# One table for the order of five engines in the layer loop of a graph network kernel

## The chip, the core and the metric

The kernel runs on one core of a Trainium2 chip. The core has five engines that work side by side: TensorE (PE in the profile, with its weight loads as PEld), VectorE (DVE), ScalarE (ACT), GpSimd (POOL) and SyncE (SP), whose work here is to issue transfers. Each engine takes its instructions strictly from its own queue. The metric is the time of one execution on the device, in microseconds; the time of a kernel is the median of its runs.

## The reference

`x` holds 128 graphs of 64 nodes with 256 features, `adj` one 64x64 matrix for each. Four layers follow each other, and each ends in `x = layernorm(x + layer(x, adj))`:

- Layer 0: five groups of nodes among the first 25, each with two graph convolutions (256 to 512 to 256), fused with softmax weights.
- Layer 1: one symmetric normalised graph convolution.
- Layer 2: a polynomial of degree 3 in the row-normalised adjacency, times a linear map, then a leaky ReLU.
- Layer 3: five rounds of message passing with a GRU cell. This is most of the work:

```python
A = (adj != 0)
for l in range(5):
    m   = einsum('bnd,de->bne', h, weight[l])
    agg = einsum('bij,bid->bjd', A, m)
    gi, gh = agg @ w_ih.T + b_ih, h @ w_hh.T + b_hh      # three gates of 256 columns
    r, z = sigmoid(i_r + h_r), sigmoid(i_z + h_z)
    n = tanh(i_n + r * h_n)
    h = (1 - z) * n + z * h
```

Everything is float32.

## The kernel before

**Chunks and steps.** The 128 graphs form 16 chunks of 8; two graphs lie together in 128 partitions, so a chunk has four such pairs. Layer 0 runs first, over all graphs, with layers 1 and 2 of chunks 0 and 1 woven in. Then comes the layer 3 loop. Two chunks are in work at a time and alternate: step s does one round of the chunk `rows[s % 2]`. Ten steps, a *period*, take two chunks through five rounds. There are 79 steps in the loop; a last one is written out behind it. In steps 8 and 9 of a period the chunks are in their last round.

**Products of a step.** The gate products use a fast scheme with seven block products instead of eight. `Gates.product(i)` issues product i; 1, 6, 7 and 4 accumulate in one PSUM bank a, 2 in bank b, 5 and 3 in bank d. Between them ACT copies bank a out (`c`, L794), and DVE adds such a copy to bank b or d (L796, L800, L806). Before product 6 can write into bank a, the copy c1 must have read it, and so on for 7 and 4. There is one such set for the gates r and z (`parz`, `pbrz`, `pdrz`) and one for n (`pan`, `pbn`, `pdn`). Products 5, 6, 7 and 4 read sums of the operands that POOL makes in `sums` (L757 to L759: `Th` of the state, `Ta` of the message).

**The rest of a step.** `sigmoid` (L871) runs on ACT; `reset` (L934, L935) on DVE, tanh (L940) on ACT, then three operations of `update` (L941 to L943) on DVE. `new(i)` does reset, tanh and update for one quarter of the state. `flip` turns half of a new state around: a DVE transpose (L918), one write to DRAM (L923), four reads back (L927), both issued by SP. `messages` gathers the neighbours on PE (L224), copies on ACT (L226) and makes `Ta`. `state_by_transfer` (L829 to L846) brings the next chunk's state into its transposed form, through DRAM as well. `output` and `close` add the result to x, normalise (L152) and store it.

**Filler.** `mid(c)` does layers 1 and 2 of a later chunk. It is a generator; each `next(filler)` in `step` issues it up to its next `yield`. There are nine pieces to a chunk, and two places for them in most steps.

**What sets the order.** In the loop PE, ACT, SP and POOL issue in the order in which `step` is written. DVE is left to the scheduler of the language, which builds a fixed order from priorities (`tc.high_priority()`) and estimates when the kernel is built. The centre of `step` is:

```python
        x.rz(1)
        if w: w.new(3)
        if closing: closing.close()
        ...
        x.rz(2); x.rz(5)
        if s % (2 * L): next(filler, None)
        x.rz(6); x.sigmoid(2)
        x.n(1); x.n(2); x.rz(7); x.new(2)
        ...
        x.rz(3)
        if w and w.l < L - 1: w.messages()
        ...
        x.sigmoid(3); x.new(7); x.n(4); x.n(3); x.new(4)
```

Of the kernel before, what the change touches and what calls it, by code (L numbers as in the profile page):

```python
# [25 lines left out]
H = CB * N // 2  # L26
# [39 lines left out]


@with_exitstack
def gnn_stack(
# [45 lines left out]
    def inv_sqrt(v, n, p, name):  # L115

        s = small.tile([p, n], F32, name=name + "s")
        nc.vector.scalar_tensor_tensor(s, v, 0.0, v, op0=ALU.is_equal, op1=ALU.add)
        r = small.tile([p, n], F32, name=name + "r")
        powers.append(nc.gpsimd.tensor_tensor(r, s, mhalf[:p, :n], ALU.pow))  # L120
        o = small.tile([p, n], F32, name=name + "o")
        nc.vector.scalar_tensor_tensor(o, v, 0.0, r, op0=ALU.not_equal, op1=ALU.mult)
        return o

# [109 lines left out]
    def mid(c, first=False):  # L234
# [3 lines left out]
        with tc.issue_after(evictions[-1].ins):  # L238
            for two in range(2):
                b = slice(two * N, (two + 1) * N)  # L240
                nc.vector.transpose(AT1[b, :, b], aB[b])
        nc.vector.tensor_scalar(A01, Ab, 0.0, None, op0=ALU.not_equal)
        rsum = small.tile([128, NP], F32, name="rsum")
        with tc.issue_after(evictions[-1].ins):
            nc.vector.tensor_reduce(rsum, Ab, AX.X, ALU.add)
        rdeg = small.tile([128, NP], F32, name="rdeg")
        nc.vector.tensor_scalar(rdeg, rsum, 1.0, None, op0=ALU.add)
        rinv = small.tile([128, NP], F32, name="rinv")
# [3 lines left out]
        nc.vector.tensor_scalar(rsum, rsum, 1e-9, None, op0=ALU.add)  # L252
        dg = keep.tile([128, NP, 128], F32, name="dg", bufs=1)
        nc.vector.tensor_mul(
            dg, ident[:, None, :].to_broadcast([128, NP, 128]), rsum[:, :, None].to_broadcast([128, NP, 128])
        )
        An = keep.tile([128, NP, 128], F32, name="An", bufs=1)
# [4 lines left out]
        poly = keep.tile([128, NP, 128], F32, tag="poly", name="poly3", bufs=2)  # L262
        nc.scalar.activation(poly, dg, AF.Identity, scale=cw[:, 2:3])
        dinv1 = inv_sqrt(rdeg, NP, 128, "d1")
        with tc.high_priority():
            nc.vector.scalar_tensor_tensor(poly, AT1, cw[:, 3:4], poly, op0=ALU.mult, op1=ALU.add)

# [5 lines left out]
        xt = xts.pop(c)  # L273
        p = psum("pp").rearrange("p (q n) -> p q n", q=NP)
        for q in range(NP):
            nc.tensor.matmul(p[:, q, :], An[:, q, :], poly[:, q, :], start=True, stop=True)
        poly = keep.tile([128, NP, 128], F32, tag="poly", name="poly1", bufs=2)
        with tc.high_priority():
            nc.vector.scalar_tensor_tensor(poly, dg, cw[:, 1:2], p, op0=ALU.mult, op1=ALU.add)
        ag = gather(halves(xt), AT1, "ag1")  # L280
        if not first:
            yield
        nc.vector.tensor_add(xt, xt, l1bs[:, None, :].to_broadcast([128, NP, D]))
        p = psum("pp").rearrange("p (q n) -> p q n", q=NP)
        for q in range(NP):
            nc.tensor.matmul(p[:, q, :], An[:, q, :], poly[:, q, :], start=True, stop=True)
        poly = keep.tile([128, NP, 128], F32, tag="poly", name="poly0", bufs=2)
        with tc.high_priority():
            nc.vector.scalar_tensor_tensor(poly, dg, cw[:, 0:1], p, op0=ALU.mult, op1=ALU.add)
        yield  # L290
        for u in range(NP // 2):
            p = psum("pd").rearrange("p (q d) -> p q d", q=2)
            for h in range(2):
                q = 2 * u + h
                for k in range(2):
                    nc.tensor.matmul(  # L296
                        p[:, h, :], ag[:, k, q * 128 : (q + 1) * 128], L1W[:, k, :], start=k == 0, stop=k == 1
                    )
            for h in range(2):
# [3 lines left out]
                )  # L303
        norm = norm_stats(xt)
        yield
        norm_apply(xt, *norm_root(*norm))
# [5 lines left out]
        for u in range(NP // 2):  # L312
            p = psum("pd").rearrange("p (q d) -> p q d", q=2)
            for h in range(2):
                q = 2 * u + h
                for k in range(2):
                    nc.tensor.matmul(
                        p[:, h, :], ag[:, k, q * 128 : (q + 1) * 128], L2W[:, k, :], start=k == 0, stop=k == 1
                    )
            v = keep.tile([128, 2, D], F32, name="v", bufs=1)  # L320
            for h in range(2):
                q = 2 * u + h
                nc.scalar.activation(v[:, h, :], p[:, h, :], AF.Identity, bias=cb, scale=rinv[:, q : q + 1])
            nc.vector.scalar_tensor_tensor(v, v, 0.2, v, op0=ALU.mult, op1=ALU.max)
            nc.vector.tensor_add(xt[:, 2 * u : 2 * u + 2, :], v, xt[:, 2 * u : 2 * u + 2, :])
        norm = norm_stats(xt)
        yield
        norm_apply(xt, *norm_root(*norm))
# [433 lines left out]
    class Gates:  # L762
# [22 lines left out]
        def product(self, i):  # L785
            C = self.C
            if i == 1:
                self.a = self.bank("a")
            if i in (1, 6, 7, 4):
                self.multiply(self.a, i)  # L790
                if i != 4:
                    c = self.copies[i] = work.tile([128, 2, H], F32, tag="copy", name=f"c{i}", bufs=4)
                    with tc.high_priority():
                        nc.scalar.copy(c, self.a)  # L794
                if i == 7:
                    nc.vector.tensor_add(C[:, :, 1, H:], self.d, self.copies.pop(7))  # L796
            elif i == 2:
                b = self.bank("b")
                self.multiply(b, i)
                nc.vector.tensor_add(C[:, :, 0, :H], b, self.copies.pop(1))  # L800
            else:
                if i == 5:
# [413 lines left out]
```

## Time and profile before

| | |
|---|---|
| median of 3 runs | 2202.35 us (2202.05 to 2204.06) |
| the profiled execution | 2206.19 us, span in the trace 2204.1 us |
| layer 0, first part of the span | up to about 345 us |
| 79 steps of layer 3 | 344.6 to 2171.3 us |
| last step and output | 2171.3 to 2204.1 us |
| mean clock granted to PE | 0.99 |

The profile is one execution. Its span reaches from the first to the last instruction; the 2.1 us between span and time lie around it. A row of the list of instructions names source line, engine, operation, the tile written and those read, a count, busy time and the mean duration of one. Behind it may stand the engine's idle time just before, with what ended it. Neighbouring matmuls overlap, so that PE's busy time is no measure of its idle moments alone; the distance from one start to the next is.

### The profile page before, as it was taken

The page shows a single profiled execution, that of the slowest core. Times are in us where ns is not written, and L with a number is a line of the kernel's source. Part 1 is how long each engine was busy: PE and PEld are TensorE (multiplying, and loading weights), DVE is VectorE, ACT ScalarE, POOL GpSimd, SP SyncE. Part 2 cuts the span into 40 slices and gives each one's busy share as a digit, 9 for nine tenths or more (in the row PEclk, how much of TensorE's full clock was granted, in tenths as well). Part 3 has the DMA queues.
Part 4 walks back from the last instruction along what each step waited for, and adds up shares of the span by engine and source line. Part 5 has one row for each costly group of instructions (what it writes and reads, how often), then busy time and mean ns, then how long its engine had stood idle before and what let it go on. Part 6 is the DMA issues. An engine that isn't in the chain of part 4 may idle for free.

```text
span 2204.1 us, 31432 instructions
## 1 busy us (share of the span) xinstructions
PE 2117.5 (96%) x10738; PEld 1832.8 (83%) x10738; DVE 1603.6 (73%) x3881; ACT 974.3 (44%) x2006; POOL 605.0 (27%) x635
## 2 busy tenths in 40 slices
PE   9989999999899999999999989999999999999997
PEld 6667788888788887888788878888888888888886
DVE  3344665777888688877887777869787788778666
ACT  3323334444444444444444444444444444454444
POOL 3311121232323213322222232323222233323222
PEclk9989999999999999999999999999999999999999
DMA  6632110222322242223331332224221332223221
GB/s 164 180 107 67 32 47 20 55 56 58 77 72 53 53 77 77 60 52 72 72 77 39 77 67 77 52 50 86 65 66 39 78 78 66 55 61 74 61 58 39
DMA packets 521994, 149.76 MB, mean 68 GB/s; under 512 B 488702, under 2 KB 516860, under 8 KB 521836
## 3 DMA queue, kind: packets, MB, share of 16 engines
q1 hardware_dynamic: 516996, 142.58, 26.6%
q0 software_dynamic: 2128, 4.77, 0.9%
q8 instruction: 85, 1.39, 0.3%
q10 hardware_dynamic: 2712, 0.42, 0.1%
q14 instruction: 73, 0.60, 0.1%
HBM read 82.67 MB, written 65.01 MB: 67 GB/s over the span
## 4 chain that ended last, share of the span: by engine, by line
PE 64%; DVE 18%; DMA 5%; SPq 4%; ACT 4%; issue 2%; POOL 2%; ACTq 0%; DVEq 0%; POOLq 0%
PE parz L777 16%; PE pan L777 9%; PE pdrz L777 8%; PE pa L224 7%; PE pdn L777 4%; PE pbrz L777 4%; PE ps L468 3%; PE ph L452 3%; DMA hb<-flip 3%; PE pd L296 3%; DVE NI L934 2%; PE pbn L777 2%; DVE RZ L941 2%; DVE NI L935 2%; DVE RZ L942 1%
## 5 line engine op out<-in xcount | busy, mean ns | idle before, releaser
L777 PE MATMUL parz<-Th,WHH 128*128 128x256 f32 x960 | 291.1, 385 | 26.5 <-ACT c L794 26.5
L940 ACT ACTIVATE NI<-NI,bih 128x256 f32<-128x256 f32 x316 | 159.9, 506 | 349.0 <-DVE NI L935 348.6
L777 PE MATMUL parz<-Ta,V 128*128 128x256 f32 x960 | 288.4, 382 | 0.0
L757 POOL TENSOR_TENSOR Ta<-agg 128x512 f32<-128x512 f32 x80 | 103.0, 1288 | 642.3 <-ACT agg L226 642.3
L794 ACT COPY c<-parz 128x512 f32<-128x512 f32 x240 | 139.5, 581 | 272.2 <-PE parz L777 272.0
L871 ACT ACTIVATE RZ<-RZ,brz 128x256 f32<-128x256 f32 x474 | 215.1, 504 | 46.1 <-DVE RZ L800 31.6
L777 PEld LDWEIGHTS parz<-Th,WHH 128*128 128x128 f32 x960 | 180.4, 192 | 57.6 <-ACT c L794 34.4
L777 PEld LDWEIGHTS parz<-Ta,V 128*128 128x128 f32 x960 | 184.5, 192 | 25.8
L140 POOL TENSOR_TENSOR rs<-ve,mhalf 128x4 f32<-128x4 f32 (+2 forms) x65 | 68.3, 1051 | 368.4 <-DVE ve L133 301.2
L757 POOL TENSOR_TENSOR Th<-hn 128x512 f32<-128x512 f32 x64 | 81.4, 1272 | 319.9 <-DVE hn L943 289.0
L226 ACT COPY agg<-pa 128x512 f32<-128x512 f32 x160 | 93.7, 586 | 162.8 <-PE pa L224 162.8
L777 PE MATMUL pan<-Ta,V 128*128 128x256 f32 x474 | 146.4, 391 | 19.4 <-ACT c L794 18.9
L794 ACT COPY c<-pan 128x512 f32<-128x512 f32 x237 | 136.4, 576 | 33.5 <-PE pan L777 32.3
L777 PE MATMUL pan<-Th,WHH 128*128 128x256 f32 x474 | 142.1, 382 | 0.0
L942 DVE TENSOR_TENSOR RZ<-RZ 128x256 f32<-128x256 f32 x316 | 139.1, 442 | 2.7
L934 DVE SCALAR_TENSOR_TENSOR NI<-NI,bhh,RZ 128x256 f32<-128x256 f32 x237 | 130.4, 550 | 4.1
L224 PEld LDWEIGHTS pa<-A,h 128*128 128x128 f32 x1024 | 126.2, 193 | 6.6 <-issue 3.0
L224 PE MATMUL pa<-A,h 128*128 128x128 f32 x1024 | 127.4, 277 | 2.5 <-DMA h<-hb 2.5
L941 DVE TENSOR_TENSOR RZ<-hn,NI 128x256 f32<-128x256 f32 x252 | 106.2, 421 | 18.4 <-ACT NI L940 17.4
L935 DVE TENSOR_TENSOR NI<-NI 128x256 f32<-128x256 f32 x237 | 113.1, 477 | 3.2
L777 PEld LDWEIGHTS pan<-Ta,V 128*128 128x128 f32 x474 | 80.7, 192 | 38.4 <-ACT c L794 32.6
L943 DVE TENSOR_TENSOR hn<-RZ,NI 128x256 f32<-128x256 f32 x256 | 108.7, 444 | 2.3
(231 smaller groups left out, 4815.2 us busy)
## 6 DMA issues: line engine op xcount, KB each, us to landing
hb<-flip SPq DMA_DIRECT2D x184, 256.0 KB
h<-hb SPq DMA_DIRECT2D x624, 64.0 KB
out_dram<-xt SPq DMA_DIRECT2D x30, 256.0 KB
hT<-hb SPq DMA_DIRECT2D x112, 64.0 KB
W<-in_w_dram SPq DMA_DIRECT2D x10, 512.0 KB
xt<-xb SPq DMA_DIRECT2D x32, 156.0 KB
xo<-in_x_dram SPq DMA_DIRECT2D x9, 512.0 KB
xb<-xo SPq DMA_DIRECT2D x9, 512.0 KB
```

What stands on the lines that cost most here:

```text
L224: nc.tensor.matmul(p[:, q * 128 : (q + 1) * 128], src(q, k), m[:, q, :], start=True, stop=True)
L226: nc.scalar.copy(a[:, k, :], p)
L757: nc.gpsimd.tensor_sub(t[:, 0:2, :], a[:, :, H:], a[:, 0, :].rearrange("p (s n) -> p s n", s=2))
L777: nc.tensor.matmul(bank[:, g, :], w[:, q, i - 1, :], rhs, start=i in (1, 2, 5) and g == 0 and m == 0, stop=m == len(side) - 1, skip_group_ ...
L794: nc.scalar.copy(c, self.a)
L871: nc.scalar.activation(v, self.g.a[:, q, :] if i == 4 else v, AF.Sigmoid, bias=brz[:, 2 * q + j : 2 * q + j + 1])
L934: nc.vector.scalar_tensor_tensor(n[:, j, f], h, bhh[:, 4 + j : 5 + j], r[:, j, f], op0=ALU.add, op1=ALU.mult)
L935: nc.vector.tensor_add(n[:, j, f], i, n[:, j, f])
L940: nc.scalar.activation(n, n, AF.Tanh, bias=bih[:, 4 + j : 5 + j])
L941: e.tensor_sub(d, self.hT[:, j, f], n)
L942: e.tensor_mul(d, d, z)
L943: e.tensor_add(self.hn[:, j, f], d, n)
```

## The change

The pieces of a step get one-letter names, and a table `ORDERS` lists them in order for each kind of step: "8", "9", "0" and "1" for those places in a period, "p" for the six others. `step` walks through the list. DVE joins the engines whose order is fixed in the loop. A capital letter is the chunk of this step (x), a small one that of the step before (w):

- R, N: gate products (r and z; n). r, n: their copies on ACT. A, B: their sums on DVE.
- S: sigmoid. X, T, U or x, t, u: reset, tanh and update, which `new` had in one. f: a flip with its write. d: the four reads.
- G: messages. e and h: POOL's sums of the state. y: state transfer. l: loads. p: one piece of filler.

`mid` yields 19 times a chunk in the loop instead of nine. Its roots on POOL, and poly3 on ACT, are issued earlier. `output` becomes a generator of four pieces, the last with the normalisation and the store, and goes ahead of `mid` at the places p. The message gather stands behind products N4 and N3 where it stood ahead of them. Both flips stand in the next step. Chunks 0 and 1, in layer 0, keep 16 places.

```diff
+ORDERS = {
+    "p": """
+u3 l u4 t7 R1 h r1 R2 p u7 R5 f0 f1 e R6 d0 y r6 A2 d1 N1 N2 n1 B2 S2 p R7 X2
+N6 r7 n6 T2 p N5 A7 S7 R4 N7 n7 U2 p R3 N4 B7 S4 A3 N3 X7 B3 S3 X4 G X3 T3 p T4
+""",
+    "8": """
+R1 t7 l u4 r1 R2 u7 A2 R5 u3 p f0 f1 R6 d0 N1 d1 N2 r6 h n1 B2 p e y S2 R7 r7
+N6 N5 p X2 n6 T2 A7 R4 N7 n7 p S7 R3 N4 B7 A3 N3 S4 G X7 X4 B3 S3 U2 X3 p T4 T3
+""",
+    "9": """
+u3 h l R1 R5 t7 R2 u7 u4 r1 A2 f0 d0 p f1 R6 r6 N1 N2 p n1 S2 d1 p B2 X2 R7 r7
+e N6 n6 N5 A7 T2 N7 y R4 S7 n7 S4 U2 p R3 B7 N4 N3 G A3 X7 S3 B3 p X4 X3 T4 T3
+""",
+    "0": """
+u4 R1 h r1 u3 t7 R2 R5 u7 p R6 f0 f1 A2 N1 r6 d0 l d1 n1 y N2 S2 R7 N6 p B2 N5
+X2 r7 n6 A7 R4 T2 N7 n7 p U2 p B7 e R3 S7 A3 X7 N4 N3 S3 S4 B3 X4 T4 G X3 p T3
+""",
+    "1": """
+u4 u3 R1 h t7 R2 R5 p u7 l f0 r1 R6 e r6 f1 d1 N1 n1 N2 A2 B2 d0 S2 p R7 r7 N6
+X2 n6 T2 N5 A7 R4 N7 n7 p U2 B7 p y R3 S7 A3 N4 S4 X7 N3 S3 G B3 X4 X3 T4 T3 p
+""",
+}
...
         rdeg = small.tile([128, NP], F32, name="rdeg")
         nc.vector.tensor_scalar(rdeg, rsum, 1.0, None, op0=ALU.add)
+        root = inv_sqrt_begin(rdeg, NP, 128, "d1")
...
         norm = norm_stats(xt)
+        norm = norm_root(*norm)
         yield
-        norm_apply(xt, *norm_root(*norm))
+        norm_apply(xt, *norm)
...
+        def copy(self, i):
+            c = self.copies[i] = work.tile([128, 2, H], F32, tag="copy", name=f"c{i}", bufs=4)
+            with tc.high_priority():
+                nc.scalar.copy(c, self.a)
+
+        def sum(self, i):
+            v = self.C[:, :, 1, H:] if i == 7 else self.C[:, :, 0, :H] if i == 2 else self.C[:, :, 0, H:]
+            nc.vector.tensor_add(v, self.b if i == 2 else self.d, self.copies.pop({7: 7, 2: 1, 3: 6}[i]))
...
+        def update(self, i):
+            j, f = self.part(i)
+            n, d, z = self.NI[:, 1, j, f], self.RZ[:, 0, j, f], self.RZ[:, 1, j, f]
+            nc.vector.tensor_sub(d, self.hT[:, j, f], n)
+            nc.vector.tensor_mul(d, d, z)
+            nc.vector.tensor_add(self.hn[:, j, f], d, n)
...
+                if q % 2:
+                    yield
+            norm = norm_stats(self.xt)
+            norm = norm_root(*norm)
+            yield
+            mv, rs, _ = norm
+            nb = small.tile([128, NP], F32, name="nb")
+            nc.vector.scalar_tensor_tensor(nb, mv[:, :, 0], -1.0, rs, op0=ALU.mult, op1=ALU.mult)
+            self.norm = mv, rs, nb
+            self.close()
+            yield
...
+    def piece():
+        while outputs:
+            try:
+                return next(outputs[0])
+            except StopIteration:
+                outputs.pop(0)
+        next(filler, None)
...
+        for o in ORDERS[{8: "8", 9: "9", 0: "0", 1: "1"}.get(s % (2 * L), "p")].split():
+            k, i = o[0], int(o[1:] or 0)
+            if k in do:
+                do[k](i)
+            elif k == "e" and w:
+                w.end()
...
+            elif k == "p":
+                piece()
...
+            elif k == "G" and w:
+                if w.l < L - 1:
+                    w.l += 1
+                    w.messages()
+                else:
+                    if nxt:
+                        nxt.messages()
+                        rows[(s + 1) % 2] = nxt
+                    outputs.append(w.output())
         before = x

-    ordered = {mybir.EngineType.Activation, mybir.EngineType.SP, mybir.EngineType.Pool}
+    ordered = {
+        mybir.EngineType.Activation, mybir.EngineType.SP, mybir.EngineType.Pool, mybir.EngineType.DVE,
+    }
```

The updates of the loop's last step that are still due stand behind the first product of the last step, as a group.

## The prediction

> **What bounds the kernel now.** I read the busy shares first, then the waits of PE, then the table of busy time by stretch for one ten-step period of layer 3, and last the timelines around the largest wait.
>
> ```profile
> PE 2117.5 (96%) x10738; PEld 1832.8 (83%) x10738; DVE 1603.6 (73%) x3881; ACT 974.3 (44%) x2006; POOL 605.0 (27%) x635
> ...
> PE parz L777 <- ACT c L794: 26.5, 17, 2.6
> PE pan L777 <- ACT c L794: 18.9, 23, 2.0
> PE pT L419 <- DVE A L411: 15.3, 2, 14.4
> PE pdrz L777 <- POOL Ta L757: 7.6, 6, 1.5
> PE pa L224 <- DMA h<-hb: 2.5, 2, 2.3
> ```
>
> PE is the bound, and what can be gained is PE's waiting (total, times, longest). Of its five lines only the third lies in layer 0. Layer 3 loses time to copies out of the accumulating bank that ACT makes late, and to POOL's sums Ta.
>
> ```profile
> 1300.38:1329.01 28.63, 24.83 (x126) 21.43 (x124) 23.43 (x56) 12.35 (x26) 10.26 (x11) 0.94 0.32 85
> ...
> 1400.02:1419.94 19.92, 19.92 (x102) 17.75 (x100) 14.77 (x32) 9.89 (x21) 6.59 (x8) 1.00 0.22 53
> ...
> sum 234.78, PE 227.54 PEld 200.84 DVE 186.22 ACT 108.26 POOL 67.69; mean PE 22.75 PEld 20.08 DVE 18.62 ACT 10.83 POOL 6.77
> ```
>
> The rows are steps 41 and 45 (length, then busy PE, PEld, DVE, ACT, POOL, then clock). Step 45 has no filler on PE and runs at PE's floor, 19.92 us. Step 41 has 2.7 us of filler products, so a floor of 22.6, and takes 28.6 at a lower clock. To size this I took all starts of matmuls from PE's timeline: 256 columns follow each other at 0.215 us, 128 columns at 0.112. Whatever a distance exceeds that by is lost. By place in the period (step number modulo 10) a step loses on average 0.9 (0), 5.0 (1), 0.8 (2), 1.4 (4) and 2.6 us (9), and nothing (under 0.06) in 3, 5, 6, 7 and 8. **Summed over steps 0 to 78 that is 83.3 us; it is the most that this change can win in the loop.**
>
> Step 51 shows the mechanism, first on PE, then ACT, then DVE:
>
> ```profile
> 1545.13 0.59 PE L777 MATMUL pbn<-hT,WHH 128*128 128x256 f32 x2
> 1548.30 1.22 PE L777 MATMUL parz<-Th,WHH 128*128 128x256 f32 x2 [2.57 <-ACT c L794]
> 1549.31 1.06 PE L777 MATMUL parz<-Ta,V 128*128 128x256 f32 x2
> ```
> ```profile
> 1543.10 0.51 ACT L940 ACTIVATE NI<-NI,bih 128x256 f32<-128x256 f32 x1 [5.38 <-DVE NI L935]
> 1545.09 2.07 ACT L152 ACTIVATE xt<-xt,nb,rs 128x256 f32<-128x256 f32 x4 [1.49 <-DVE nb L144]
> 1547.07 0.70 ACT L263 ACTIVATE poly<-dg,cw 128x512 f32<-128x512 f32 x1
> 1547.68 0.56 ACT L794 COPY c<-parz 128x512 f32<-128x512 f32 x1
> ```
> ```profile
> 1543.63 0.42 DVE L941 TENSOR_TENSOR RZ<-hT,NI 128x256 f32<-128x256 f32 x1 [0.57 <-ACT NI L940]
> 1544.09 0.43 DVE L942 TENSOR_TENSOR RZ<-RZ 128x256 f32<-128x256 f32 x1
> 1544.56 0.43 DVE L943 TENSOR_TENSOR hn<-RZ,NI 128x256 f32<-128x256 f32 x1
> ```
>
> ACT's queue is fixed. The copy that frees bank a for product 7 stands behind a tanh that waits for DVE, four normalisations of a finished chunk that wait for DVE's nb, and poly3. PE stops for 2.6 us.
>
> [...] the pairs after this wait start 1.01, 0.85 and 0.86 us apart instead of 0.43, some 1.8 us more. [...] here dependent L941, L942, L943 start 0.46 apart and independent ones 0.335, so only dependence costs. [...] the mean L934 is 550 ns against 470 where POOL is idle, and over a step's 20 gate operations the means exceed the quiet values by about 0.8 us.
>
> **The change, part by part.** No engine gains or loses an instruction; orders alone differ. So PE's floor stays.
>
> Filler in small pieces: a chunk of layers 1 and 2 becomes 19 pieces and an output 4, 46 per period, for 50 places (5 "p" per step). Pieces fall in a fixed sequence, so each step's load follows. A DVE base step is 12.95 us (busy in step 73, no filler); four updates as uninterrupted triples add (0.46-0.335)x2 x4 = 1.0, of which I count 0.5 since old orders held some too: 13.4. Pieces, from their rows: half an output 4x0.26 = 1.05; statistics 4x(0.32+0.08)+0.16 = 1.75; A01 1.27; row sums 1.5; dg and An 1.67; d1o and poly 0.9; AT 1.5; power 0.73; bias 1.2; product half 0.88; apply 4x0.32 = 1.3; leaky half 1.5; state transfer 1.3. DVE's load beside PE's floor (19.92 plus 1.72 per product half, 1.8 per gather, 0.9 per power) in steps 0 to 9:
>
> - 0: 18.7 / 19.9; 1: 19.5 / 19.9; 2: 17.8 / 22.6; 3: 18.9 / 24.2; 4: 18.2 / 25.2
> - 5: 20.1 / 19.9; 6: 17.6 / 23.5; 7: 18.2 / 25.2; 8: 20.8 / 23.4; 9: 15.8 / 19.9
>
> Before, DVE worked 23.4 us in step 1, 23.0 in step 4. Now only 0, 1 and 5 are full, and step 9 comes before 0 with 4 us free.
>
> Deadlines: with PE's marks (R 1.72 us, N 0.86, message gather 1.8), order p needs product 7's copy before R4 at 12.0, so S2 ahead of it needs A2 by 10.4; and n7 before N4 at 16.3, so S7 ahead of it needs A7 by 14.5. DVE enters each step late: B3 waits for N3 at 18.1, and B3 0.65, X4 0.85, X3 0.85 and a last piece of 1.7 end at 22.1, 2.2 us into the next step. Summed on from there (u3 u4 2.5, piece, u7 1.25, flips 1.3, A2 0.65) A2 ends at 8.8 in step 2 and 9.2 in step 5; B2, A01, X2, row sums and A7 end at 14.1 in step 5. The spare is 0.4 to 1.6 us, and POOL's locks, 0.8 a step, eat it over two steps running. I take 0.5 lost after step 1 and 1.3 in 5 and 6; the ends are 0 and 3 each.
>
> Closing: normalise and store sit in a piece behind n7, no longer ahead of c6. The 2.1 us on ACT now lie in front of S7, S3, S4 and the message copies: in step 0 these end at 21.2 against 20.4 wanted, 0.8 us, and 0.2 in step 1. The two output transfers wait on SP behind the period's fetches, with nothing behind them until the next step's flips.
>
> Roots (POOL's pow) start one piece before their reader: covers the 46.2 and 41.9 us of DVE waits on POOL d1r and rs, off PE's path, counted in the above.
>
> State transfer y: that of step 49 had its write issued by SP only at 1522.14, 8 us into step 50, and hT landed at 1535.17, when POOL's Th, then Ta, ran late. Now it follows A7 in step 9, about 13 us in; 13 us later is 6 to 7 us into step 0. POOL's queue there holds Th (2.9 us), so Ta of the message at 20 is not behind it: the 1.5 us waits go.
>
> Flips and fetches: SP issues both writes, then both reads. From the first flip: 0.4 + 0.4, 2.2 to land, 4 reads 1.8, again 1.8, landing 1.9 (a late gather at 2046.68 after issue ended 2044.82) = 8.4. First flip at 8.6 makes 17.0 against the gather at 18.1: hidden. If DVE is a further microsecond late, nothing hides it.
>
> Messages move behind N4 and N3: 1.72 us less cover for Ta. Gather end + copy 0.8 + Ta 1.3 to 1.4 = 2.2, needed at 3.9: hidden, except in step 9, where R5 precedes R2 (needed at 2.15): 0.2.
>
> Banks: R1 follows B2's bank, R2 S4's, N5 A2's, all earlier than the copies. Layer 0 keeps its 16 places, and the tail does three updates (3.8 us) under 7 us of products: 0, at most 2 us either way.
>
> Left over: 7 periods x (0.8+0.2+0.5+1.3+0.2 = 3.0) = 21, slow clock after these about 1: **22 us. Gain 83.3-22 = 61.** The profiled execution took 2206.2 (span 2204.1, 2.1 around it), so 2145; the median stands 3.8 lower: 2141.
>
> **Rivals.**
> 1. Nothing is left of the waits (spare is larger than I sum, since POOL's locks are already in my means): 2202.4-83.3 = 2119. For it: seven steps in ten have margin; against: step 5 holds 20.1 in 19.9.
> 2. The arrears of the full steps carry on: 1, 5 and 6 lose 2 more each, 7x6 = 42: gain 19, 2183.
> 3. **Slower.** DVE's order is fixed, and nothing passes a waiting instruction. In orders p and 9 the copy n7 stands on ACT behind S7, and S7 behind A7 on DVE, which follows X2 and a piece. If that chain reaches N4 late in ordinary steps too, 7 steps in 10 pay, 55 in all. It decides from 83.3/55 = 1.5 us per step; with 2.0 it is 110-83 = 27 slower, 2229. For it: the spare of step 5 is 0.4; against: steps 2, 4, 6, 7 and 9 have 4 to 7 us free.
> 4. The flips' reads land after the gather: a delay of 0.5 in 79 steps is 40, gain 43 - 22 = 21, 2181.
>
> **How the numbers follow.** Forecast (2125 to 2165) 0.60, rival 1 0.15, rivals 2 and 4 together 0.14, rival 3 0.09, no change 0.02. The 80% range leaves out rival 3 and half a tail of 1: 2119 to 2183. Faster by over 0.2% (4.4 us, about what a measurement of this kernel can tell from no change) 0.89, within 0.02, slower 0.09.
>
> **What would show it.** Right: steps 0, 1, 5 and 9 take 20 to 21.5 us and 2 to 4 and 6 to 8 their floors above; parz's wait on c falls below 5 us, pdrz's on Ta below 2; the state transfer's write is issued inside step 9. Wrong: waits of pan on c in every step (rival 3), of pa on h<-hb (rival 4), or parz on ACT agg in all steps.

## The result, and the profile after

In this measurement the kernel before took 2203.2 us (median of 4 runs, 2202.05 to 2204.68), the changed one **2172.67 us** (4 runs, 2170.48 to 2174.68). The ratio is 0.9861, 95% interval 0.9844 to 0.9878. The gain is 30.5 us, half of the 61 us forecast. The time lies 8 us above the forecast's own range (2125 to 2165), inside the 80% range (2119 to 2183), and 8 to 10 us below the numbers of rivals 4 and 2 (2181 and 2183).

The page of the changed kernel, busy shares first, and its waits of PE (total, times, longest):

```profile
PE 2109.4 (97%) x10738; PEld 1825.9 (84%) x10738; DVE 1708.3 (79%) x3881; ACT 980.6 (45%) x2006; POOL 600.4 (28%) x635
```
```profile
PE pT L464 <- DVE A L456: 14.7, 1, 14.7
PE pdrz L822 <- DVE RZ L846: 11.9, 14, 1.6
PE pdn L822 <- DVE NI L846: 8.7, 14, 2.2
PE pan L822 <- ACT c L842: 4.6, 6, 0.8
PE parz L822 <- ACT agg L255: 3.7, 6, 0.9
PE parz L822 <- ACT c L842: 2.9, 3, 2.2
```

Instruction counts are those of before. The two waits on copies, 26.5 and 18.9 us, are down to 2.9 and 4.6; the wait on Ta (7.6) and the one on the flips' reads (2.5) are gone. In their place stand waits that before did not have: `pdrz` and `pdn` on DVE's sums. These are products R3 and N3, which write bank d and must wait until the sums A7 and B7 have read it. Line numbers have shifted: L777 is now L822, the copies are L842, the sums L846, reset L977 and L978, update L940 to L942.

The table of busy time by stretch, for steps 41, 45 and 50 (length, then busy PE, PEld, DVE, ACT, POOL):

```profile
1285.89:1305.80 19.91, 19.91 (x102) 17.74 (x101) 18.61 (x48) 10.71 (x23) 7.76 (x8) 1.00 0.30 80
1378.26:1399.28 21.02, 20.46 (x102) 17.50 (x101) 20.31 (x52) 10.22 (x21) 7.61 (x8) 1.00 0.21 51
1492.43:1515.00 22.57, 20.46 (x103) 17.58 (x102) 21.30 (x48) 11.68 (x25) 6.89 (x7) 1.00 0.58 123
```

Step 41, which took 28.6 us, is at PE's floor. Step 45 lost nothing before and now loses 1.1. Step 50, place 0 of its period, loses 2.6.

Counted as in the prediction (distance between starts of matmuls beyond 0.215 or 0.112 us; one of 256 columns is listed with 0.38 us, as neighbours overlap), the loop loses 47 us instead of 83. By place in the period, averages: 2.8 (0), 0.7 (1), 0.1, 0.1, 0.3, 0.8 (5), 0, 0.1, 0, 1.1 (9). From the first to the last step the loop is 35.9 us shorter. The tail behind it, from step 79 on, takes 36.9 us instead of 32.8. Together that is the 31.8 us between the spans 2204.1 and 2172.3.

### The profile page after: what moved, and what is told of

The parts are those of the page before. It is cut to its first block, busy times and chain, and to the rows that moved or that the text cites. A ratio compares the mean times of both kernels' runs of the same rounds, so it can differ in the third digit from the quotient of the medians.

```text
span 2172.3 us, 31481 instructions
## 1 busy us (share of the span) xinstructions
PE 2109.4 (97%) x10738; PEld 1825.9 (84%) x10738; DVE 1708.3 (79%) x3881; ACT 980.6 (45%) x2006; POOL 600.4 (28%) x635
## 4 chain that ended last, share of the span: by engine, by line
PE 76%; DVE 14%; DMA 3%; POOL 2%; ACT 2%; SPq 2%; issue 1%; POOLq 0%; DVEq 0%; ACTq 0%
PE parz L822 19%; PE pdrz L822 10%; PE pan L822 10%; PE pa L253 8%; PE pdn L822 5%; PE pd L323 5%; PE pbrz L822 5%; PE ps L513 4%; PE ph L497 3%; PE pbn L822 2%; DVE xt L184 2%; DVE NI L977 1%; DVE RZ L940 1%; PE pp L312 1%; DVE RZ L941 1%
## 5 line engine op out<-in xcount | busy, mean ns | idle before, releaser
L842 ACT COPY c<-parz 128x512 f32<-128x512 f32 x240 | 138.4, 577 | 365.3 <-PE parz L822 365.3
L802 POOL TENSOR_TENSOR Ta<-agg 128x512 f32<-128x512 f32 x80 | 111.4, 1393 | 693.2 <-ACT agg L255 693.2
L822 PE MATMUL parz<-Th,WHH 128*128 128x256 f32 x960 | 286.8, 380 | 2.9 <-ACT c L842 2.9
L822 PE MATMUL parz<-Ta,V 128*128 128x256 f32 x960 | 286.0, 380 | 0.0
L822 PEld LDWEIGHTS parz<-Th,WHH 128*128 128x128 f32 x960 | 180.8, 190 | 29.5 <-ACT c L842 2.7
L822 PEld LDWEIGHTS parz<-Ta,V 128*128 128x128 f32 x960 | 182.7, 190 | 24.9
L935 ACT ACTIVATE NI<-NI,bih 128x256 f32<-128x256 f32 x316 | 148.7, 503 | 98.1 <-DVE NI L978 96.1
L842 ACT COPY c<-pan 128x512 f32<-128x512 f32 x237 | 138.1, 583 | 105.3 <-PE pan L822 105.3
L941 DVE TENSOR_TENSOR RZ<-RZ 128x256 f32<-128x256 f32 x316 | 157.4, 498 | 10.7
L846 DVE TENSOR_TENSOR NI<-pdn,c 128x512 f32<-128x512 f32 x158 | 108.6, 687 | 55.3 <-ACT c L842 47.7
L940 DVE TENSOR_TENSOR RZ<-hn,NI 128x256 f32<-128x256 f32 x252 | 128.4, 509 | 26.8 <-ACT NI L935 26.6
L822 PE MATMUL pan<-Ta,V 128*128 128x256 f32 x474 | 141.7, 381 | 4.6 <-ACT c L842 4.6
L822 PE MATMUL pan<-Th,WHH 128*128 128x256 f32 x474 | 141.0, 379 | 0.0
L977 DVE SCALAR_TENSOR_TENSOR NI<-NI,bhh,RZ 128x256 f32<-128x256 f32 x237 | 126.4, 533 | 8.2 <-ACT RZ L920 5.0
L846 DVE TENSOR_TENSOR RZ<-pdrz,c 128x512 f32<-128x512 f32 x160 | 109.5, 685 | 29.0 <-PE pdrz L822 24.2
L942 DVE TENSOR_TENSOR hn<-RZ,NI 128x256 f32<-128x256 f32 x256 | 120.6, 471 | 9.1
```

The costliest lines, as they stand in the source:

```text
L802: nc.gpsimd.tensor_sub(t[:, 0:2, :], a[:, :, H:], a[:, 0, :].rearrange("p (s n) -> p s n", s=2))
L822: nc.tensor.matmul(bank[:, g, :], w[:, q, i - 1, :], rhs, start=i in (1, 2, 5) and g == 0 and m == 0, stop=m == len(side) - 1, skip_group_ ...
L846: nc.vector.tensor_add(v, self.b if i == 2 else self.d, self.copies.pop({7: 7, 2: 1, 3: 6}[i]))
L935: nc.scalar.activation(n, n, AF.Tanh, bias=bih[:, 4 + j : 5 + j])
L940: nc.vector.tensor_sub(d, self.hT[:, j, f], n)
L941: nc.vector.tensor_mul(d, d, z)
```

## What is left of the waits: POOL's sums stretch DVE

Step 50 shows how the 2.6 us come about. DVE at the step's start, then POOL, in the changed kernel:

```profile
1493.66 1.19 DVE L977 SCALAR_TENSOR_TENSOR NI<-NI,bhh,RZ 128x256 f32<-128x256 f32 x1 [0.22 <-ACT RZ L920]
1494.88 0.83 DVE L978 TENSOR_TENSOR NI<-NI 128x256 f32<-128x256 f32 x1
1495.63 0.95 DVE L940 TENSOR_TENSOR RZ<-hn,NI 128x256 f32<-128x256 f32 x1
1496.62 0.43 DVE L941 TENSOR_TENSOR RZ<-RZ 128x256 f32<-128x256 f32 x1
```
```profile
1493.29 1.27 POOL L802 TENSOR_TENSOR Ta<-agg 128x512 f32<-128x512 f32 x1 [15.25 <-ACT agg L255]
1494.64 0.79 POOL L803 TENSOR_TENSOR Ta<-agg,Ta 128x256 f32<-128x256 f32 x1
1495.51 0.79 POOL L804 TENSOR_TENSOR Ta<-agg,Ta 128x256 f32<-128x256 f32 x1
```

Three DVE operations stand beside POOL's three, and each ends about 0.3 us after the POOL operation that it met. They take 2.97 us instead of 1.32 (0.48, 0.42, 0.42 below). DVE has no wait in which to make this up: from 1493.66 to 1508.63, where A7 ends, it is busy for 14.4 of 15.0 us. Just ahead of A7 it loses 1.2 us more beside POOL's Th (a 128x4 operation of the statistics takes 0.98 us instead of 0.17, a reset sum 0.83 instead of 0.42). PE waits 1.41 us for A7.

Two experiments settle that POOL's sums are the cause. In the first POOL makes no sums at all; in the second it makes them and nobody reads them:

```python
def sums(a, name): return None                      # no_sums
rhs = {..., 4: a[:, 1, :H], 5: a[:, 0, H:], 6: a[:, 1, H:], 7: a[:, 1, :H]}[i]   # both
```

**no_sums.**

> The changed kernel without POOL's sums Th and Ta (products 4 to 7 read the operand's own halves instead, so the outputs are not the reference's): POOL is left with the pow operations alone, and PE, ACT and DVE do the same number of instructions in the same order. Theory P (what is left of PE's waits comes from POOL: its sums keep DVE's two-input operations and the normalisations waiting, and so DVE enters steps 0, 1, 5 and 9 late): lost time in the loop falls from 47 us to below 15, gate operations all at 0.42 to 0.48, about 2135 to 2145 us. Theory O (the arrears come from the order itself: S3 behind the message copies, a piece ahead of X4 and X3, the writes behind the reads): lost time stays above 35 us, 2160 to 2172.

Measured: 2139.2 us (4 runs), ratio to before 0.9703 (0.9688 to 0.9717); 16 us lost in the loop, tail 33.6. Theory P holds: the time is in its range, the loss just above the 15 us that it allowed. DVE in the same place of step 50 of this kernel (L973, L974, L936 are the same three operations):

```profile
1473.39 0.48 DVE L973 SCALAR_TENSOR_TENSOR NI<-NI,bhh,RZ 128x256 f32<-128x256 f32 x1 [0.22 <-ACT RZ L916]
1473.91 0.42 DVE L974 TENSOR_TENSOR NI<-NI 128x256 f32<-128x256 f32 x1
1474.25 0.42 DVE L936 TENSOR_TENSOR RZ<-hn,NI 128x256 f32<-128x256 f32 x1
```

**sums_unread.**

> The changed kernel with POOL's sums Th and Ta written but not read (products 4 to 7 read the operand's own halves, so the outputs are not the reference's). POOL works as much and at about the same places as in the changed kernel, but no product waits for it. Theory K (POOL's sums cost by what they do to DVE[...]): like the changed kernel, 2165 to 2175 us, loss in the loop over 40 us. Theory D (products wait for Ta and Th, directly or by the order behind them): like the kernel without sums, 2138 to 2148.

Measured: 2173.6 us (4 runs), 0.9856 (0.9842 to 0.9871), over 50 us lost in the loop. It is the changed kernel again, waits included:

```profile
PE pdrz L822 <- DVE RZ L846: 11.5, 14, 1.7
PE pdn L822 <- DVE NI L846: 10.1, 13, 3.8
PE pan L822 <- ACT c L842: 4.6, 6, 0.8
```

Theory K holds: no product waits for Ta or Th, directly or behind something else, and the 34 us between the two runs come from POOL's work. It could cost in one other way: on POOL's queue the roots (pow) stand behind the sums, and DVE waits for roots. In the loop it does so for 6.5 us in the changed kernel, 8.1 in sums_unread and 0.9 in no_sums. Against that, DVE is busy for 1197.6 us in steps 10 to 69 of the changed kernel and for 1093.3 in no_sums, with the same instructions. So the stretched operations are by far the larger part.

Which operations suffer is seen in the groups of DVE's instructions with shapes kept apart (busy us, then mean ns). First the changed kernel, then no_sums:

```profile
L941 DVE TENSOR_TENSOR RZ<-RZ 128x256 f32<-128x256 f32 x316 | 157.4, 498 | 10.7
L977 DVE SCALAR_TENSOR_TENSOR NI<-NI,bhh,RZ 128x256 f32<-128x256 f32 x237 | 126.4, 533 | 8.2 <-ACT RZ L920 5.0
L184 DVE TENSOR_SCALAR xt<-xt,mv,rs 128x256 f32<-128x256 f32 x130 | 71.2, 608 | 6.5 <-POOL rs L169 5.7 <-POOL rs L1031 0.8
L977 DVE SCALAR_TENSOR_TENSOR NI<-pan,bhh,RZ 128x256 f32<-128x256 f32 x79 | 37.5, 475 | 0.0
```
```profile
L937 DVE TENSOR_TENSOR RZ<-RZ 128x256 f32<-128x256 f32 x316 | 134.2, 425 | 10.7
L973 DVE SCALAR_TENSOR_TENSOR NI<-NI,bhh,RZ 128x256 f32<-128x256 f32 x237 | 113.3, 478 | 12.5 <-ACT RZ L916 9.4
L184 DVE TENSOR_SCALAR xt<-xt,mv,rs 128x256 f32<-128x256 f32 x130 | 44.8, 407 | 6.5 <-POOL rs L169 5.6 <-POOL rs L1027 0.9
L973 DVE SCALAR_TENSOR_TENSOR NI<-pan,bhh,RZ 128x256 f32<-128x256 f32 x79 | 37.6, 476 | 0.1
```

The reset with both inputs in SBUF takes 478 ns on average without POOL's sums and 533 with them; in the changed kernel the 35 that overlap a sum take 862, the 202 others 476. The one that reads its input from PSUM (`pan`) takes 475 to 476 ns in both, but there none overlaps a sum. Before, 68 of its 79 did: these take 479 ns, the 11 others 470. The normalisation L184 has one large input and goes from 407 to 608. Why one form is stretched and another not, the runs don't show. What the prediction and the expectations call POOL's lock is this stretch.

I summed it: for each DVE instruction in the loop that overlaps one of POOL's sums, its duration less the median of its own kind beside no sum. That gives 66 us under Ta and 26 under Th before, and **112 and 22 in the changed kernel**, together 1.7 us a step. The change raised it without one instruction more. These are groups of before, to set beside L184, L941 and L977 above: the normalisation and the update's product have grown, the reset has not.

```profile
L155 DVE TENSOR_SCALAR xt<-xt,mv,rs 128x256 f32<-128x256 f32 x130 | 46.4, 407 | 42.7 <-POOL rs L140 41.9 <-POOL rs L996 0.8
L942 DVE TENSOR_TENSOR RZ<-RZ 128x256 f32<-128x256 f32 x316 | 139.1, 442 | 2.7
L934 DVE SCALAR_TENSOR_TENSOR NI<-NI,bhh,RZ 128x256 f32<-128x256 f32 x237 | 130.4, 550 | 4.1
```
The reason is where the sums lie. Before, the gather stood ahead of N4 and N3, and Ta ran beside reset 4 (from PSUM), sum B3 (from PSUM) and the transposes (0.48, 0.68 and 0.71 us on average beside a sum, 0.47, 0.68 and 0.70 beside none). Now Ta runs over reset 3, the updates and the normalisations.

**gather_early** tests that reason. The gather is put back ahead of N4 in all five sequences, all else as changed; sequence p:

```diff
-R3 N4 B7 S4 A3 N3 X7 B3 S3 X4 G X3 T3 p T4
+R3 G N4 B7 S4 A3 N3 X7 B3 S3 X4 X3 T3 p T4
```

> The message gather goes back ahead of N4 and N3 in all five orders; all else stays. Theory G (the late gather costs: the agg copy waited for in step 1, R5 in step 9, and POOL's Ta lies on the updates at the next step's start): the wait of parz on ACT agg (3.7 us) goes and DVE's operations are blocked less, 4 to 10 us faster, 2163 to 2169. Rival H (the late gather is needed for the fetched state): waits of pa on h<-hb appear, 0.3 to 0.8 us a step, 2190 to 2220. My own prediction had the move at nearly nothing: within 4 us of 2172.7.

Measured: 2196.8 us (12 runs), 0.9973 (0.9964 to 0.9982); 75 us lost in the loop. The stretch falls to 34 us under Ta and 20 under Th, so the gather's place does set it. But rival H holds, and neither theory G nor my own prediction, for PE now waits elsewhere; its waits in this kernel:

```profile
PE pa L253 <- DMA h<-hb: 14.0, 8, 2.6
PE pdrz L822 <- DVE RZ L846: 10.9, 14, 1.7
PE parz L822 <- ACT c L842: 8.6, 20, 1.1
```

Of the 14.0 us of waits on the flips' reads 13.8 lie in step 1 of the periods. The late gather gives the reads and the copies their time and is worth 24 us in all, although it puts Ta over DVE's worst operations.

**g_mid** puts G between N4 and N3 in sequence p, that is in steps 2 to 7 (`N4 B7 S4 A3 N3 X7 B3 S3 X4 G X3` becomes `N4 B7 S4 A3 G N3 X7 B3 S3 X4 X3`).

> The changed kernel with the message gather of sequence p (steps 2 to 7) between N4 and N3 rather than behind N3, 0.9 us earlier. Ta then lies over B3 and X4, which read PSUM, and the locks of these steps fall (over all steps 112 us of stretched DVE operations under Ta, 34 with the gather ahead of N4). If lock and reads are both as I read them, steps 2 to 7 gain little, as they lose only 1.45 us between them, and the earlier gather meets the flips' reads in some: between 3 us faster and 8 us slower than the changed kernel. If the gather's late place is worth what it is (24 us) mainly in p steps: over 10 us slower.

Measured: 2187.1 us, 0.9925 (0.9911 to 0.994), 14 us worse than the changed kernel. The stretch under Ta fell to 80 us as expected, yet the loss rose, most in step 5 (0.8 to 1.9): the second case of the expectation holds. The reads are not the reason here, PE waits only 0.9 us for them. The gather now stands ahead of N3, so N3 and its sum B3 end 1.8 us later, and DVE enters the next step that much later: A2 ends 12.4 us into step 5 instead of 10.5, and PE waits for it with product N5, whose bank it frees. B3 of step 44 in the changed kernel:

```profile
1376.68 0.69 DVE L846 TENSOR_TENSOR NI<-pdn,c 128x512 f32<-128x512 f32 x1 [0.18 <-PE pdn L822]
```

and in g_mid, with the new wait of PE:

```profile
1387.24 0.69 DVE L846 TENSOR_TENSOR NI<-pdn,c 128x512 f32<-128x512 f32 x1 [1.97 <-PE pdn L822]
PE pdn L822 <- DVE RZ L846: 6.4, 6, 1.1
```

So a part of what the late gather is worth is that it lets N3, and with it DVE, go first.

## What the gain lives from

**dve_free** takes DVE out of the fixed order again: `ordered = {Activation, SP, Pool}`, with table and pieces as changed.

> The changed kernel with DVE's order given back to the scheduler; ACT, SP, POOL and PE keep the table's order and the small pieces. Theory L (the fixed DVE order makes DVE's load per step larger, 14.9 us instead of 12.9 in a step without filler, since dependent operations stand next to each other): the step without filler falls back to about 13.0 us of DVE and the loop's lost time from 47 us to below 30, so some 2150 to 2158 us. Rival F (fixing DVE's order is what won the 30 us): the waits of ACT's copies come back, 2185 to 2205 us.

Measured: 2205.6 us (20 runs), 1.001 (1.0003 to 1.0016). The whole gain is gone, as rival F said. The cause is one place per period: step 1 loses 8.4 us on average, 67 of the 81 us lost in the loop. ACT in step 51 of this kernel:

```profile
1531.03 2.08 ACT L181 ACTIVATE xt<-xt,nb,rs 128x256 f32<-128x256 f32 x4 [5.94 <-DVE nb L1071]
1533.01 1.69 ACT L920 ACTIVATE RZ<-RZ,brz 128x256 f32<-128x256 f32 x4
```

The scheduler puts the statistics of the chunk being closed late, and nb with them. ACT's order is fixed, so ACT stands 5.9 us before four normalisations, and sigmoids and message copies behind them; PE then waits 7.2 us in one piece. Theory L (DVE's base step falls) is refuted: a step without filler has 15.3 us of DVE here, 14.9 in the changed kernel. Yet all other places together lose 13 us in the loop, against 41 in the changed kernel. The scheduler takes work out of the full step 0 (17.4 us of DVE instead of 21.5), and PE pays for it in step 1. How much of the 28 us can be had is open, since the long stop also lets DVE catch up; fixing the place of the statistics and nb alone, with the rest of DVE free, wasn't tried.

**before_fixed** is the other half alone: the kernel before with `ordered = {Activation, SP, Pool, DVE}`, and nothing else.

> The kernel before with one edit: VectorE's order is fixed too, in the order in which its code is written; no table, no small pieces. If fixing DVE's order is by itself worth anything (the statistics and nb then come where they are written), parz's wait on the copies falls and it is 5 to 20 us faster than before. If the table is what puts the fixed order right, a DVE operation waiting at the head of its queue stops everything behind it, and it is slower than before by over 20 us. I expect the second.

Measured: 2376.4 us, 1.0779 (1.0761 to 1.0797). The fixed order by itself costs 172 us: with no table, each DVE operation that waits holds up all behind it. At the head of its queue DVE now stands 239 us in the loop before updates that wait for a tanh, where it was 25 us.

**coarse** keeps table and fixed order, and gives `mid` its nine pieces back (`if not first: yield` removed; filler at the second and fifth p only).

> The changed kernel with layers 1 and 2 in nine pieces per chunk again instead of 19, taken at the second and fifth place of a step only (two a step, as before); orders of the rest, and the four pieces of an output, unchanged. If small pieces are what the change lives from (DVE then has no long stretch ahead of a deadline), lost time in the loop goes back above 70 us, 2195 or more. If the fixed order and the late places of closing and messages are what counts, it loses 5 to 12 us against the changed kernel: 2178 to 2185.

Measured: 2205.1 us (12 runs), 1.0007 (0.9998 to 1.0015); 79 us lost in the loop. The first of the two cases holds: it is 32 us worse than the changed kernel, with 24.5 us of waits of `parz` on the copies as before. So the parts don't add up. With DVE free, or with large pieces, the whole gain is gone; DVE fixed without the rest is far worse than before. Table and small pieces with DVE free are dve_free; the fixed order with small pieces but without the table wasn't tried, nor were the earlier roots, the closing in pieces or the later flips alone.

## Trials at what is left

**nine_s3** changes the end of sequence 9:

```diff
-R3 B7 N4 N3 G A3 X7 S3 B3 p X4 X3 T4 T3
+R3 B7 N4 N3 A3 S3 G X7 B3 X4 X3 T4 T3 p
```

> The changed kernel with the end of sequence 9 rewritten: A3 S3 stand ahead of G (so that the sigmoid S3 is ahead of the message copies on ACT), and the last piece stands behind X3 and T3. Theory O: X3 of step 9 no longer waits for S3 and is over before POOL's Ta begins to hold DVE, the updates of step 0 start 1.5 us sooner, and step 0's loss falls from 2.8 to about 1.0: 8 to 12 us faster than the changed kernel, 2161 to 2165. Theory P: POOL's Ta takes the next operations instead; step 0 keeps over 2 us, within 4 us of the changed kernel.

Measured: 2174.4 us, 0.9861 (0.9847 to 0.9876); step 0 still loses 2.7, where it lost 2.8. The order of S3 and the copies is not it. That Ta stretches the next operations instead, as theory P says, fits this.

**h_mid** moves h in sequence 9 (to the place of e, which does nothing there, as the chunk before is in its last round); **h_late** does that, moves h behind r7 in 0 as well, and y in 9 from behind N7 to behind the first p, ahead of d0 and d1:

```diff
-u3 h l R1 ... R7 r7 e N6
+u3 l R1 ... R7 r7 h N6
```

> The changed kernel with one piece moved: h of sequence 9 (the new state's sums Th) stands behind X2 and r7 instead of at the step's start, so that Ta and Th no longer run back to back over DVE's normalisation of layer 2; y and sequence 0 stay as they are. If that lock in step 9 is what makes it and step 0 late: step 9's loss 1.07 to below 0.4 and step 0's 2.76 to about 1.5, 6 to 14 us faster than the changed kernel. If step 0's own Ta (0.9 to 3.9 us into the step, over the updates) decides: within 4 us of it.

> The changed kernel with two edits around the new chunk's state: in sequences 9 and 0, h (its sums Th on POOL) stands behind X2 and r7 in the middle of the step rather than at its start, and in 9 the state transfer y follows the first piece, ahead of the reads d0 and d1 on SP. If Th directly behind Ta at the start of step 9 (5.9 us of POOL, a normalisation stretched from 1.3 to 3.7 us) and the late hT in step 0 (12.3 us in, with the pow operations behind it on POOL's queue) are what makes steps 9, 0 and 1 lose, they fall from 1.07, 2.76 and 0.74 to below 0.5, 1.5 and 0.5: 10 to 18 us faster than the changed kernel. If it is the order of DVE alone (or locks wherever Th stands), within 4 us of it.

Measured: h_mid 2174.9 us, 0.9869 (0.9855 to 0.9884), step 9 unchanged at 1.1. The edit moved nothing: on POOL's queue no instruction lies between Ta and Th, so Th starts behind Ta wherever the list names it. Whether a gap there would help wasn't tried. h_late is a miss of my own: 2211.0 us, 1.0025 (1.0013 to 1.0036). The first output piece stands at the end of sequence 9 and needs reads d0 and d1, which now queue behind the state transfer on SP. DVE stood 6.7 us before that piece with everything else behind it, and PE up to 5.9.

**pairs** interleaves updates 3 and 4 in sequences p, 0 and 1 (both subtractions, both products, both sums):

```diff
-u3 l u4 t7 R1 h r1 R2 p u7 ...
+l v t7 R1 h r1 R2 p u7 ...
```

> In orders p, 0 and 1 the updates u3 and u4 are interleaved: both differences, both products, both sums. Same instructions. Theory L: 4 of 6 distances fall from 0.46 to 0.335 us, 0.5 us less DVE in 8 of 10 steps; DVE busy in a step without filler from 14.94 to about 14.4, lost time in steps 0, 1 and 5 down by 0.5 each, together 8 to 12 us: 2160 to 2165. Rival W (single waits behind ACT decide, DVE has slack): within 3 us of 2172.7.

Measured: 2169.5 us, 0.9848 (0.9833 to 0.9864). Step 5's loss falls from 0.8 to 0.5, step 0 stays at 2.8. The median is 3.2 us lower, but the intervals overlap; the 8 to 12 us that I expected of it did not come, and rival W (within 3 us) is nearer.

**balance** moves places for pieces, here steps 3 and 4 (p added) and step 0 (p taken; the same with `T2 p N5` in step 5):

```diff
-R3 N4 B7 S4 A3 N3
+R3 N4 B7 S4 p A3 N3
-N7 n7 p U2 p B7 e
+N7 n7 p U2 B7 e
```

> The changed kernel with places for pieces moved, nothing else: step 0 of a period has four places instead of five, step 5 four, steps 3 and 4 six, so that of layers 1 and 2 no piece falls into step 0, the normalisation that stood in step 4 and 5 comes earlier, and step 5 keeps four pieces. DVE's load without locks goes from 18.3 to 17.0 in step 0 and from 19.75 to 18.45 in step 5; steps 3 and 4, with 4 us of room, take 1.3 more. If what is left is DVE's load plus lock against PE's floor of 19.9 (20.8 + 0.7 in step 0, as the trace shows it), step 0's loss falls from 2.8 to about 1.2, step 5's from 0.8 to below 0.2, step 1's from 0.7 to 0.4: 12 to 19 us faster than the changed kernel, 2154 to 2161. If the lock delays A7 and B3 in step 0 whatever the load, it is within 4 us of it.

Measured: 2180.8 us, 0.9888 (0.9865 to 0.991): 8 us slower than the changed kernel, where I expected 12 to 19 us faster. Step 0's loss falls from 2.8 to 1.6, so its load counts. But step 4 now loses 1.4, step 5 1.2 and step 1 1.1: pieces now follow each other more closely, and in step 4 the gather of layer 2 waits for the normalisation one place ahead of it (`pa` on DVE xt, 6 times, 2.5 us).

**The tail.** In the changed kernel PE waits 2.2 us for the copy of product 1 in step 79, which stands on ACT behind a tanh that waits for reset 3; four pairs of matmuls then start 0.81 to 0.86 us apart instead of 0.43, at a granted clock of 0.51 (1.00 in the 0.94 us before them). tail_plain took `tc.high_priority()` away from the tail's updates; tail_order fixed the order of its first part as written; tail_two wrote that order by hand, with the copy of product 6 ahead of S2:

```diff
-    rz(1)
-    with tc.high_priority(): ...
-    rz(2)
-    for i in (6, 5, 7): rz(i)
-    w.turn(1)
+    with tc.manual_schedule(engines=ordered):
+        x.g.product(1); x.g.copy(1); w.update(4); w.tanh(7); w.update(3)
+        x.g.product(2); w.update(7); x.g.sum(2)
+        x.g.product(5); x.g.product(6); x.g.copy(6); x.last_rz(2)
+    w.turn(1)
+    rz(7)
```

> The group of leftover updates behind the loop loses its high priority; nothing else changes. In the trace of the changed kernel the last step waits 2.16 us for a copy on ACT that stands behind a tanh, whose reset DVE took after two of those updates, and PE then runs at half clock for six pairs. Theory T (the priority let the updates pass the reset X3): this wait goes, 4 us less, 2168 to 2169. Rival: the updates are as late as the copy allows anyhow and the transposes of the old chunk wait for them instead: within 1 us of 2172.7.

> The changed kernel with the first part of the tail (product 1, its copy, the four updates of step 78, product 2) in the order as written rather than placed by the scheduler, and product 5 ahead of 6. X3 of step 78 then goes ahead of the updates on DVE, the copy of product 1 is made before product 6 wants its bank, and the one wait of 2.2 us with its slow clock is gone: the stretch from step 79's start to the end falls from 36.9 to 33 to 34 us, 3 to 4 us faster than the changed kernel. If the locks of POOL's last Ta are the whole of it, it stays at 36 to 37.

> The changed kernel with the tail's first part as written by hand: R1, its copy, update 4, tanh 7, update 3, R2, update 7, A2, R5, R6 and its copy ahead of S2, and two transposes between products 6 and 7. The wait of 2.2 us (and the 2.7 us into which the earlier order of the tail turned it, since r6 stood behind S2 and S2 behind four updates) goes: the stretch from step 79 to the end 33 us rather than 36.9, 3 to 4 us faster than the changed kernel. If a lock or the transposes take its place, 0 to 2 us.

Measured: tail_plain 2173.9 us (0.9869, 0.9849 to 0.989), the same wait, so its 4 us did not come. In its profile the slow pairs are missing and the tail takes 35.4 us, 1.5 less than the changed kernel's 36.9; four pairs that are each 0.38 to 0.43 us late add up to 1.6. tail_order 2175.6 (0.9866, 0.9852 to 0.9881): its 3 to 4 us did not come either, as the wait moved to product 7, 2.7 us, whose bank waited for a copy behind S2, and S2 for four updates. tail_two shortens the tail to 33.8 us, by 3.1 or, against a tail without slow pairs, by 1.6, but its median of 2173.5 (0.986, 0.9844 to 0.9876) doesn't show it: in its profile step 0 lost more, and 3 us are near what these intervals tell.

**best1, best2, best3** combine: pairs with h_late and the tail of tail_order (2206.9 us, 1.0012, 1.0003 to 1.002); pairs, balance and tail_two (2172.3 us, 0.9849, 0.9829 to 0.9869); and pairs, tail_two and of balance only the piece moved from step 0 to step 3. The first two miss both of their cases: best1 carries the fault of h_late, best2 the new losses of balance.

> h_late, tail_order and pairs (updates 3 and 4 interleaved) together. If the three gains add (10 to 18, 3 to 4, 3): 2148 to 2157 us. If h_late brings nothing, 2164 to 2168.

> balance, updates 3 and 4 interleaved (pairs) and the tail by hand (tail_two) together. If their gains add (12 to 19, 3, up to 3): 2148 to 2156 us. If balance brings nothing: 2166 to 2170.

> Updates 3 and 4 interleaved (pairs), the tail by hand (tail_two), and of balance only what paid: step 0 has four places for pieces instead of five, and step 3 takes the piece that is missing, so that steps 4 to 9 keep the pieces that they have in the changed kernel. In balance step 0's loss fell from 2.8 to 1.6 and steps 1 to 3 together rose by 0.3, while 1.5 us of new loss arose in steps 4 and 5, where pieces were moved too. If those two are separate: 7 us faster than pairs from step 0, up to 3 from the tail, 2160 to 2165 us. If step 1 and 4 take the piece's lateness over in any case, 2167 to 2171.

Measured: best3 **2167.6 us** (5 runs, 2167.0 to 2169.5), 0.9826 (0.9813 to 0.984). It is the fastest, 5 us below the changed kernel; the two intervals to before just miss each other (0.984 and 0.9844). Step 0 loses 1.7 as hoped; step 4 takes 1.4 over in this kernel too, so it is the second case that holds (2167 to 2171), not the 2160 to 2165 that I gave for the case that the two are separate.

## Why the prediction was half right

- **What bounds: right.** No engine's instructions changed. The 83.3 us of waits were all that the loop could give, and it gave 36. PE's floors came out: 22.7, 24.3, 25.4, 23.5, 25.2 and 23.4 us in steps 2 to 4 and 6 to 8 (means of steps 10 to 69), at most 0.2 above the forecast. Steps 1, 5 and 9 took 20.7, 21.0 and 21.1, within the 20 to 21.5 that I named; step 0 took 23.3.
- **The mechanism of step 51: right.** With the normalisation behind n7, parz's wait on the copies fell from 26.5 to 2.9 us (below 5, as stated), and pdrz's wait on Ta went. Step 1's average loss went from 5.0 to 0.7, where I had 0.2 of closing and 0.5 of arrears. dve_free shows that this hangs on nb's fixed place.
- **DVE's table: near, without POOL's sums.** In no_sums DVE's busy time in steps 0 to 9 (means over steps 10 to 69) is 18.3, 18.5, 18.0, 18.6, 17.5, 19.8, 18.4, 19.0, 17.5 and 16.8, and 13.5 in a step without filler; I had 18.7, 19.5, 17.8, 18.9, 18.2, 20.1, 17.6, 18.2, 20.8 and 15.8, and 13.4: right to 1 us except step 8, which I had 3.3 too high, without harm, as PE's floor there is 23.4. My deadlines hold there too, nearly: A2 ends 8.9 us into step 2 and 10.0 into step 5, where I had 8.8 and 9.2.
- **The term that failed: "POOL's locks, 0.8 a step".** I took it from before, from the gate operations alone. With all kinds of operations it was already 92 us in 79 steps, 1.2 a step, and the change raised it to 134 us, 1.7. The loads become 21.5 in step 0, 19.8 in 1, 20.3 in 5 and 20.0 in 9, so four steps of the period are full and not three, and A2 ends at 11.0 in step 2 and 10.5 in step 5. I named the stretch, and did not ask over which operations Ta would lie once the gather had moved. Its price is the 34 us between no_sums and sums_unread. That no_sums, at 2139.2 us, lands beside my 2141 is luck in part: my 22 us of loss had POOL's stretch in them, and it loses 16 without.
- **Left over, 3.0 a period: 6.0 measured.** Step 5 and 6: 1.3 forecast, 0.8 found. Step 1 as above. Step 0: 0.8 forecast, 2.8 found. Step 9: 0.2 against 1.1. Over eight steps 0 and seven steps 9 these two are 22 of the 25 us missed. In step 9, which I counted as the one with 4 us to spare, four normalisations under Ta and Th take 3.7 us instead of 1.3:

```profile
1474.51 3.69 DVE L184 TENSOR_SCALAR xt<-xt,mv,rs 128x256 f32<-128x256 f32 x4
```

- **Deadlines I left out.** I listed the copies of products 7 and n7. What PE waits for most in layer 3 are R3 and N3 on A7 and B7. That the banks are "all earlier than the copies" was wrong here: A7 and B7 come late in exactly the full step.
- **State transfer: forecast at half its time.** I had the write 13 us into step 9 and hT landing 6 to 7 us into step 0. In step 50 it lands 12.3 us in (POOL's Th starts at 1504.69): SP issues the write only at 1492.25, 21 us into step 49, behind reads d0 and d1. From write to landing it takes 12.4 us, where I had 13. PE did not stop for it; Th then stretched A7's neighbours by 1.2 us.
- **Messages: wrong price.** "hidden, except in step 9" was my whole account of the move: it is worth 24 us, by the time that it leaves to reads and copies and by letting N3 go first.
- **Tail: "0, at most 2 us either way"**: 4.1 us longer. tail_two brings 3.1 of it back; the four pairs at a clock of 0.51 made about 1.5 of these in the profile of the changed kernel, and the copy's place the rest.
- **Rivals.** The numbers of rivals 4 (2181) and 2 (2183) are nearest from above, but neither came about. Arrears did not carry on from 1 to 2 and from 5 to 6; the loss is in step 0. Rival 3 (n7's chain) and rival 4 (reads after the gather) did not happen; gather_early shows that rival 4 was close: with the gather 1.7 us earlier, 14.0 us of waits on the flips' reads appear.
- **Slips in the sums.** The flips' times add up to 8.5, not 8.4. Step 0 comes eight times in the loop, and I counted seven periods. The reset L934 takes 478 ns on average where it meets no sum, not 470. None of them matters for the 30 us that are missing.

## What to carry to other kernels

When an order is moved, ask of each POOL operation which DVE operations will now run beside it: in these traces an operation with one input from PSUM paid 0.01 us at most on average there (the reset, 479 and 470 ns), and one with two inputs in SBUF up to 1.1 us. Fixing an engine's order paid here only with an order made for it, pieces small enough to fit its gaps, and a check of every queue; a name moved in a list moves nothing on a queue that has no instruction between the two places. Ask also which product stands behind the piece that is moved, and what that product feeds. If deadlines are listed, list the banks of the later products too, not only the copies.

## What the runs showed of the hardware

- One DVE operation with 256 columns and both inputs in SBUF takes 0.42 us (0.48 for the reset's first) beside none of POOL's sums, and 0.74 to 0.91 on average, by source line, beside one of them, at most 1.5. The sums L846, with one input from PSUM, take 0.65 to 0.69 either way; the statistics L159 0.39 and 0.40.
- It is not only a matter of two inputs: the normalisation L184, one tensor and two columns, takes 0.41 and 1.02.
- The same wait of PE of 2.2 us, in step 79, is followed by four pairs of matmuls at a granted clock of 0.51, 0.81 to 0.86 us apart, in the profile of the changed kernel and by none in that of tail_plain, where the tail takes 35.4 us instead of 36.9.
- POOL's sums are stretched too. The bias addition L335 takes 1.22 us beside a sum as without one, and the sum that starts 0.13 to 0.14 us after it, six times in the loop, takes 2.20 to 2.22 instead of 1.27. DVE and POOL of the changed kernel:

```profile
1329.33 1.22 DVE L335 TENSOR_TENSOR xt<-xt,l1bs 128x1024 f32<-128x1024 f32 x1
```
```profile
1329.46 2.21 POOL L802 TENSOR_TENSOR Ta<-agg 128x512 f32<-128x512 f32 x1 [10.86 <-ACT agg L255]
```

In sum POOL pays less: its sums take 465 us, and would take 433 if each had the shortest duration of its kind, which is 32 us against DVE's 134.
